# Gates written in place and staged ahead of the residual steps; in the scan, the last states' carry folded in by ScalarE and one product divided by columns

## The chip, the cores and the metric

The kernel runs on one core of a Trainium2 chip. The time is device microseconds (us) of one execution; lower is better. The core's engines are TensorE (PE, with its weight loads as PEld), VectorE (DVE), ScalarE (ACT) and GpSimd (POOL), each with its own queue of instructions in a fixed order, and SyncE (SP), which issues most DMAs. Engines meet only at semaphores.

## The reference

An input x of 2 x 128 x 64 x 64 goes through four layers; the change touches layer 1's end, layer 2 and layer 3.

```python
# layer 1, its end
d = (out - out.mean((2, 3))) ** 2
out = out * sigmoid(d / (4 * (d.sum((2, 3)) / n + 1e-4)) + 0.5) + x      # the gate
# layer 2
for _ in range(3):
    t = relu(conv3x3(x, w1) + b1)
    x = x + (conv3x3(t, w2) + b2) / 3
x = relu(x)
# layer 3: four directions over the pixels (rows, columns, each forward and backward)
dt = softplus(...); dA = exp(dt * A)           # 256 channels x 16 states x 4096 steps
dBu = dt * B * u
h[t] = dA[t] * h[t-1] + dBu[t]                 # the scan
y = sum over states of h * C, + u * D, * silu(z), @ W_out
out = x + fuse(y of the four directions)
```

## The kernel before, in words

**The gate, layer 1 to 2.** `gate` (L918) makes one part of an image: a DMA brings the part of x (`xr`) from `g.xs`, ScalarE does Square (L923) and Sigmoid (L924) into `e`, VectorE multiplies by the fused image (L925), and VectorE (image 0) or GpSimd (image 1) adds x and writes the sum by columns of four into `first` (L926), which lies in the memory of `v[1][b]`. `gated(b, k)` (L1030) calls it for part k of image b (17, 16, 16 and 15 rows), and then `differences` (GpSimd, L1009 and L1010) and `combine` (VectorE, ten operations, L1019 to L1028), which make six transformed inputs `v[0][b]` from the four columns. All four parts of image 0 come first, then `settle(0)` (ScalarE copies `first` to `image`, L1044), `quad_weights` (ten VectorE operations on the second weights) and the residual steps.

**The residual steps, layer 2.** `block(step, j, b, k)` (L1046) is one half image of one convolution: 36 matmuls into six of eight PSUM banks, L1052; then two ScalarE copies, ten VectorE operations (L1060 to L1072), a relu, and the `combine` of the block that went before it (`due`). Step 0, convolution 0 has four such blocks; the gates of image 1 stand behind the blocks of image 0, two parts behind each.

**The scan, layer 3.** 64 blocks (2 images, 4 directions, 8 pieces of 512 steps; called i) each have 8 groups k = (hf, ng): a half of the channels and four of the sixteen states. A group holds four units q, each 128 x 512. In the order of a group: `db_dve` (L1413) and `db_pool` (L1422) make `db` = B times dt*u, VectorE `ND[hf][ng]` of the four units, from PSUM, and GpSimd the rest; `expo` (L1430) is ScalarE's exp into `da`, one of three PSUM banks, two units ahead of the scan (`AHEAD`); `scan` (L1439) is VectorE's scan in place on `db`, whose initial value is the column `hl` that the same group left in the block before, or 0.0 in the first block of a direction; `keep` (L1444, ScalarE) saves the last column to `hl`; `cmul` (L1449, GpSimd) multiplies by C; `sums` (L1457, TensorE) adds up the states. Between groups ScalarE has the work of the next block: two table loads and two silus at the end of slot 7 (L1300, L1301) and of slot 4 (L1313, L1314), two copies at the end of slot 0 (L1325, L1327), softplus at the end of slots 1 and 2. A group's place in its block, 0 to 7, is its slot. All of this is in an order written out by hand (`manual_schedule`).

Of the kernel before, what the change touches and what calls it, by code (L numbers as in the profile page):

```python
# [20 lines left out]
P = 128  # L21
# [925 lines left out]
def layer2(g, I):  # L947
# [14 lines left out]
    with ExitStack() as ctx:  # L962
# [8 lines left out]

        mid = [a.tile([P, 4, RP, NS], F32, name=f"mid{i}") for i in range(2)]

        raw = mid[1].rearrange("p c r i -> p (c r i)")[:, : 9 * P]
        nc.sync.dma_start(raw, I["w2T"].rearrange("p t o -> p (t o)"))
        u2 = a.tile([P, 3, NX, P], F32, name="u2")
        weights = (g.u1, u2)
# [32 lines left out]
            nc.gpsimd.tensor_sub(t[1], d[5], d[3])  # L1010
            return t

        def combine(dst, at, src, r0, n, t):
# [5 lines left out]
            stt(o[2], d[2], -4.0, d[4], ALU.mult, ALU.add)  # L1019
            stt(h, d[1], -4.0, d[3], ALU.mult, ALU.add)  # L1020
            nc.vector.tensor_add(o[1], o[2], h)  # L1021
            nc.vector.tensor_sub(o[2], o[2], h)
            nc.vector.tensor_sub(d42, d[4], d[2])
# [6 lines left out]
        def gated(b, k):  # L1030

            r0, r1 = (0, 17, 33, 49, 64)[k : k + 2]
            n = r1 - r0
            dst = first[b][:, :, r0:r1, 0:NQ]
            if g.gates:
                t = wk.tile([P, 2, 17 * HW], F32, name="gt")
                gate(g, b, r0, n, t[:, 0, : n * HW], t[:, 1, : n * HW], dst, by_column, nc.gpsimd if b else nc.vector)
            else:
                nc.vector.tensor_copy(dst, interior(g, b, r0, n).rearrange("p r (i c) -> p c r i", c=4))
            places = [v[0][b][:, x, 1 + r0 : 1 + r1, :] for x in (0, 5)]  # L1040
            combine(v[0][b], r0, first[b], r0, n, differences(first[b], r0, n, places))

        def settle(b):
            nc.scalar.copy(image[b], first[b])  # L1044

        def block(step, j, b, k):  # L1046
            m = {}
            for x in (1, 2, 3, 4, 0, 5):
                m[x] = ps.tile([P, BLK], F32, name="m")
                for dy in range(3):  # L1050
                    r0 = k * RP + dy
                    nc.tensor.matmul(  # L1052
                        m[x], weights[j][:, dy, x, :], v[j][b][:, x, r0 : r0 + RP, :].rearrange("p r i -> p (r i)"),
                        start=(dy == 0), stop=(dy == 2),
                    )
            s, p = (wk.tile([P, BLK], F32, name=f"m{i}", bufs=2) for i in range(2))
# [12 lines left out]
            stt(d, q, 8.0, d, ALU.mult, ALU.add)  # L1069
            nc.vector.tensor_add(s, s, p)  # L1070
            nc.vector.tensor_add(y[0], rows_of(s), rows_of(m[0]))
            nc.vector.tensor_add(y[3], rows_of(d), rows_of(m[5]))  # L1072
            xv = image[b][:, :, k * RP : (k + 1) * RP, 0:NQ]
            if j == 0:
                nc.scalar.activation(inner(t), inner(t), AF.Relu)
                where = (v[1][b], k * RP, t, 0, RP)
            elif step < 2:
                nc.vector.tensor_add(xv, xv, inner(t))
                where = (v[0][b], k * RP, image[b], k * RP, RP)
            else:  # L1080
# [5 lines left out]
                where = None  # L1086

            if due:
# [6 lines left out]
        with tc.manual_schedule():  # L1095
            for b in range(NB):
                nc.gpsimd.memset(first[b][:, :, :, NQ:], 0.0)
                for e in (0, HP - 1):
                    nc.gpsimd.memset(v[0][b][:, :, e, :], 0.0)
            nc.gpsimd.memset(mid[0][:, :, :, NQ:], 0.0)  # L1100
            for k in range(4):
                gated(0, k)
            settle(0)
            quad_weights(g, u2, raw.rearrange("p (y x o) -> p y x o", y=3, x=3), 1.0 / 3.0)
            nc.gpsimd.memset(mid[1][:, :, :, NQ:], 0.0)
            for step in range(3):
                for j in range(2):
                    for b in range(NB):
                        if step == 0 and j == 0:
                            for e in (0, HP - 1):  # L1110
                                nc.gpsimd.memset(v[1][b][:, :, e, :], 0.0)
                        for k in range(NK):
                            block(step, j, b, k)
                            if step == j == b == 0:
                                gated(1, 2 * k)
                                gated(1, 2 * k + 1)
                        if step == j == b == 0:
                            settle(1)


def layer3(g, I, out):
# [5 lines left out]
    nc, tc = g.nc, g.tc  # L1127
    NJ = 4

    ND = ((4, 0, 1, 4), (4, 4, 0, 4))  # L1130
    NNG = N_STATE // NJ
    HB = 1
    HC = 3
    with ExitStack() as ctx:
# [259 lines left out]

        def copies(i, x, ng):

            if x == "b" and ND[0][ng] == ND[1][ng] == 4:
# [11 lines left out]
        def db_dve(k):  # L1409
            i, hf, ng = groups[k]  # L1410
            n = ND[hf][ng]
            if n:
                nc.vector.tensor_tensor(  # L1413
                    db_tile(k)[:, :n, :], G[k].pop("pb").unsqueeze(1).to_broadcast([P, n, BLK]),
                    S[i]["d4", hf][:, 1, :n, :], ALU.mult,
                )

        def db_pool(k):
            i, hf, ng = groups[k]
            n = ND[hf][ng]  # L1420
            if n < 4:
                nc.gpsimd.tensor_tensor(  # L1422
                    db_tile(k)[:, n:, :], S[i]["b", ng].unsqueeze(1).to_broadcast([P, 4 - n, BLK]),
                    S[i]["d4", hf][:, 1, n:, :], ALU.mult,
                )

        def expo(k, q):
            i, hf, ng = groups[k]
            da = psd.tile([P, BLK], F32, name="da")
            nc.scalar.activation(da, S[i]["d4", hf][:, 0, q, :], AF.Exp, scale=am[:, hf, q, ng : ng + 1])  # L1430
            G[k]["da", q] = da

        def scan(k, q):
            i, hf, ng = groups[k]
            d0, d1 = G[k].pop(("da", q)), G[k]["db"][:, q, :]
            if reverse(i):
                d0, d1 = d0[:, ::-1], d1[:, ::-1]
            first = i % NBLK == 0
            nc.vector.tensor_tensor_scan(d1, d0, d1, 0.0 if first else hl[:, hf, ng, q, :], ALU.mult, ALU.add)  # L1439

        def keep(k):
            i, hf, ng = groups[k]
# [124 lines left out]
        with tc.manual_schedule():  # L1567
# [62 lines left out]
            for k in range(len(groups) + 7):  # L1630
# [221 lines left out]
```

## Time and profile before

| what | value |
|---|---|
| median of 3 runs | 5816.95 us (5814.35 to 5819.41) |
| profiled execution, its own time | 5815.21 us |
| its span, mean granted TensorE clock | 5813.4 us, 0.889 |
| busy: PE, DVE, ACT, POOL | 84%, 76%, 66%, 62% of the span |
| layer 2: first VectorE operation on a gate's sum, last matmul's end | 2017.37 us, 2441.92 us |
| layer 3: first scan, last scan's start | 2500.78 us, 5796.04 us |

A duration is that of one instruction. Two instructions that follow each other on an engine can overlap by some 0.08 to 0.1 us, so what an instruction costs its engine is the time from its start to the next one's. "idle before" is time in which the engine waited, with what ended the wait.

### The profile page before, as it was taken

Reading aid. Unit: us, or ns where it says so; the run is one execution under the profiler, and the core shown is the slowest. Engines: PE = TensorE matmul, PEld = TensorE weight load, DVE = VectorE, ACT = ScalarE, POOL = GpSimd, SP = SyncE. Lnnn points to the kernel's source line nnn. Section 1 sums busy time; section 2 is a strip of 40 time slices with the busy share of each in tenths; the row PEclk is TensorE's granted clock in tenths of the full one; section 3 lists DMA queues with packets and bytes.
Section 4 is the critical chain, followed back from the end, with each engine's and each line's share of the span. In section 5 each row is a group of like instructions: output and inputs, shape, how many; then the busy total and the mean of one; then the engine's idle time right before and its main releaser. Section 6 shows DMA issues by size and latency. Waiting matters only on the chain.

```text
span 5813.4 us, 57554 instructions
## 1 busy us (share of the span) xinstructions
PE 4881.1 (84%) x19110; PEld 1732.0 (30%) x19110; DVE 4427.0 (76%) x4138; ACT 3827.3 (66%) x5499; POOL 3620.8 (62%) x1136
## 2 busy tenths in 40 slices
PE   7999999989978779977787777787788877777776
PEld 3333333334434334422222222222222222222221
DVE  5333333356124589779999999999999999999998
ACT  4888888850025521277777777777777777777775
POOL 5111111110010031179999999999999999999998
PEclk8999999999989889988888888888888888888886
DMA  5000001030046300065555555556655555555554
GB/s 157 19 19 19 19 19 33 1 60 1 1 90 121 74 18 0 6 143 128 135 130 131 143 140 129 128 130 148 145 129 136 127 134 143 139 129 135 132 139 102
DMA packets 333105, 541.88 MB, mean 93 GB/s; under 512 B 66384, under 2 KB 121184, under 8 KB 331712
## 3 DMA queue, kind: packets, MB, share of 16 engines
q1 hardware_dynamic: 329664, 534.58, 39.5%
q10 hardware_dynamic: 3136, 3.56, 0.2%
q8 instruction: 151, 2.47, 0.2%
q14 instruction: 154, 1.26, 0.1%
HBM read 448.81 MB, written 89.13 MB: 93 GB/s over the span
## 4 chain that ended last, share of the span: by engine, by line
DVE 50%; PE 37%; issue 4%; POOL 3%; DMA 3%; ACT 2%; SPq 1%; DVEq 0%; POOLq 0%; ACTq 0%
DVE db L1439 35%; DVE db L1413 11%; PE ps L287 11%; PE acc L303 9%; PE m L1052 6%; PE m L566 5%; PE acd L812 2%; DVE gt L1466 1%; PE m L526 1%; POOL db L1449 1%; POOL db L1422 1%; PE pf L775 1%; PE pc L663 1%; DMA c<-bx 1%; SPq L748 1%
## 5 line engine op out<-in xcount | busy, mean ns | idle before, releaser
L1449 POOL TENSOR_TENSOR db<-db,c 128x2048 f32<-128x2048 f32 x512 | 2310.8, 4532 | 36.5 <-ACT hl L1444 33.8
L1439 DVE TENSOR_TENSOR_SCAN db<-da,hl,db 128x512 f32<-128x512 f32 x1792 | 2154.7, 1263 | 40.4 <-ACT da L1430 3.5
L1430 ACT ACTIVATE da<-dd,am 128x512 f32<-128x512 f32 x2048 | 1402.2, 689 | 803.4 <-DVE db L1439 794.1
L293 ACT ACTIVATE e<-ps 128x1024 f16<-128x1024 f32 x1024 | 992.2, 1021 | 134.5 <-PE ps L287 117.2
L1422 POOL TENSOR_TENSOR db<-b,dd 128x2048 f32<-128x2048 f32 (+1 forms) x192 | 799.8, 4166 | 13.3 <-DMA b<-bx 13.3
L1457 PE MATMUL py<-db,fold 128*32 128x512 f32 x4096 | 618.0, 689 | 223.9 <-POOL db L1449 220.9
L1413 DVE TENSOR_TENSOR db<-pbc,dd 128x2048 f32<-128x2048 f32 (+1 forms) x384 | 766.5, 1996 | 32.0 <-DMA dd<-dx 32.0
L314 DVE RECIPROCAL rec<-acc 32x512 f32<-32x512 f32 x64 | 214.9, 3358 | 639.0 <-PE acc L303 612.1
L321 POOL TENSOR_TENSOR parts<-parts 32x512 f32<-32x512 f32 x64 | 80.4, 1257 | 975.1 <-DVE parts L320 975.1
L287 PE MATMUL ps<-q,k 32*128 32x512 f32 x4096 | 656.0, 643 | 3.5 <-DVE flag L250 2.7
L303 PE MATMUL acc<-e,v 128*128 128x512 f16 x2048 | 531.3, 382 | 0.0
L1052 PE MATMUL m<-v,u 128*128 128x512 f32 x864 | 376.1, 598 | 51.7 <-DVE v L1021 51.7
L1360 PE MATMUL pm<-dd,ident 128*128 128x512 f32 x512 | 356.6, 834 | 2.9 <-ACT dd L1353 2.7
L1392 PE MATMUL pbc<-bc,sel 64*128 64x512 f32 x384 | 207.5, 540 | 153.5 <-DVE db L1413 152.9
L1319 PE MATMUL pm<-u,wxp 128*72 128x512 f32 x256 | 189.4, 882 | 155.2 <-ACT u L1300 155.2
L303 PEld LDWEIGHTS <-v 128*128 128x128 bf16 x2048 | 158.5, 97 | 509.6 <-issue 388.3
L287 PEld LDWEIGHTS ps<-q,k 32*128 32x128 f32 x4096 | 229.7, 183 | 227.9 <-issue 146.2
L1439 DVE TENSOR_TENSOR_SCAN db<-da,db 128x512 f32<-128x512 f32 x256 | 292.3, 1202 | 6.2 <-ACT da L1430 1.3
L1457 PEld LDWEIGHTS py<-db,fold 128*32 128x32 f32 x4096 | 90.5, 114 | 607.0 <-POOL db L1449 356.4
L566 PE MATMUL m<-comb,w 64*128 64x512 f32 (+4 forms) x1296 | 269.9, 575 | 0.0
L1295 PE MATMUL pm<-xt,wcs 128*128 128x512 f32 x512 | 235.6, 602 | 24.6 <-ACT xa L1484 15.4
L686 POOL TENSOR_SCALAR yt<-y 32x512 f32<-32x512 f32 x8 | 18.2, 2271 | 381.7 <-DVE y L677 381.4
(318 smaller groups left out, 6031.8 us busy)
## 6 DMA issues: line engine op xcount, KB each, us to landing
dd<-dx SPq DMA_DIRECT2D x1024, 256.0 KB, 6.4
dx<-dd SPq DMA_DIRECT2D x128, 512.0 KB, 5.4
c<-bx SPq DMA_DIRECT2D x1024, 64.0 KB, 2.1
hats<-pos SPq DMA_DIRECT2D x136, 256.0 KB, 9.5
b<-bx SPq DMA_DIRECT2D x512, 64.0 KB, 4.5
q<-qd SPq DMA_DIRECT2D x32, 512.0 KB, 7.4
w<-in_conv0T SPq DMA_DIRECT2D x18, 288.0 KB, 8.6
q<-in_x SPq DMA_DIRECT2D x8, 512.0 KB, 7.2
```

Source lines behind the costliest of these rows:

```text
L287: nc.tensor.matmul(ps[:, i, :], k4[h % 2][rows, kb // 4, :], q4[h % 2][rows, qb * BLK : (qb + 1) * BLK], start=True, stop=True,)
L293: nc.scalar.activation(e[:, :n, :], ps[:, :n, :], AF.Exp)
L303: nc.tensor.matmul(acc, v3[b][:, kb, h, :], e[:, i, :], start=(kb == 0), stop=(kb == NS - 1))
L566: yield lambda q=q, dy=dy, src=src, i0=i0, i1=i1: nc.tensor.matmul(m[:, i0 * NF : i1 * NF], w[half, dy, q, x, :], src, start=(dy == KC and ...
L1052: nc.tensor.matmul(m[x], weights[j][:, dy, x, :], v[j][b][:, x, r0 : r0 + RP, :].rearrange("p r i -> p (r i)"), start=(dy == 0), stop=(dy ...
L1360: nc.tensor.matmul(ps, g.ident, S[i]["dd", hf][:, x, :], start=(x == 0), stop=(x == 1))
L1413: nc.vector.tensor_tensor(db_tile(k)[:, :n, :], G[k].pop("pb").unsqueeze(1).to_broadcast([P, n, BLK]), S[i]["d4", hf][:, 1, :n, :], ALU.mult,)
L1422: nc.gpsimd.tensor_tensor(db_tile(k)[:, n:, :], S[i]["b", ng].unsqueeze(1).to_broadcast([P, 4 - n, BLK]), S[i]["d4", hf][:, 1, n:, :], ALU ...
L1430: nc.scalar.activation(da, S[i]["d4", hf][:, 0, q, :], AF.Exp, scale=am[:, hf, q, ng : ng + 1])
L1439: nc.vector.tensor_tensor_scan(d1, d0, d1, 0.0 if first else hl[:, hf, ng, q, :], ALU.mult, ALU.add)
L1449: nc.gpsimd.tensor_mul(v, v, S[i]["c", ng].unsqueeze(1).to_broadcast([P, 4, BLK]))
L1457: nc.tensor.matmul(S[i]["y", hf][32 * q : 32 * q + 32, :], fold, G[k]["db"][:, q, :], start=False, stop=(ng == NNG - 1),)
```

## The change

**Layer 1 to 2.** `gate`'s steps become `gate_weight` (the DMA into `gt`; Square and Sigmoid, which now read the image by columns of four and write straight into `first`), `gate_product` (VectorE, in place), `gate_sum` (adds x from `gt`; VectorE for part 0 of image 0, GpSimd for all others), `gate_differences` and `gate_combine`. `combine` takes a `between`: a product of a later part, put behind its fourth operation. `block` is divided into `products` (matmuls), `outputs` and `later` (the `combine` that is due). The order of the first four blocks and the eight parts is written out; `quad_weights` comes behind the third block's outputs. The second weights are loaded into the upper end of `v[1][1]` in place of `mid[1]`. `gate` itself is left for a case that doesn't occur here.

**Layer 3.** For the units q = 2 and 3 of every group, and for all four of the groups whose `db` GpSimd makes alone, except in a direction's first block, ScalarE adds `da[first] * hl` to the first column of `db` right behind `expo`, and the scan starts from 0.0. These are 20 of a block's 32 units, 56 blocks: 1120. `ND` counts columns instead of units: in group (0, 2) VectorE makes columns 0 to 175 of all four units in place of one whole unit. `keep(k - 1)` moves ahead of `expo(k, 2)`.

```diff
-        raw = mid[1].rearrange("p c r i -> p (c r i)")[:, : 9 * P]
+        raw = v[1][1].rearrange("p x r i -> p (x r i)")[:, 4 * HW * NS : 4 * HW * NS + 9 * P]
...
+        at = (0, 17, 33, 49, 64)
+        gt = wk.tile([P, 2, 17 * HW], F32, name="gt")
+        def gate_weight(b, k):
+            r0, n, dst, fu = part(b, k)
+            nc.sync.dma_start(gt[:, k % 2, : n * HW], g.xs[b][:, r0 * HW : (r0 + n) * HW])
+            nc.scalar.activation(dst, fu, AF.Square, bias=g.stat[:, b, 0:1])
+            nc.scalar.activation(dst, dst, AF.Sigmoid, bias=g.half, scale=g.stat[:, b, 1:2])
...
+        def gate_product(b, k):
+            _, _, dst, fu = part(b, k)
+            if g.gates:
+                nc.vector.tensor_mul(dst, dst, fu)
...
+        def gate_sum(b, k, eng):
+            _, n, dst, _ = part(b, k)
+            if g.gates:
+                eng.tensor_add(dst, dst, by_column(gt[:, k % 2, : n * HW]))
...
+            for k in range(2):
+                gate_weight(0, k)
+            gate_product(0, 0)
+            gate_sum(0, 0, nc.vector)
+            gate_product(0, 1)
+            t0 = gate_differences(0, 0)
+            gate_sum(0, 1, nc.gpsimd)
+            t1 = gate_differences(0, 1)
+            gate_weight(0, 2)
+            gate_weight(0, 3)
+            gate_combine(0, 0, t0)
+            gate_combine(0, 1, t1, (0, 2))
+            m00 = products(0, 0, 0)
+            gate_sum(0, 2, nc.gpsimd)
+            t2 = gate_differences(0, 2)
+            gate_weight(1, 0)
+            gate_combine(0, 2, t2, (0, 3))
...
+            w00 = outputs(0, 0, 0, 0, m00)
+            m01 = products(0, 0, 1)
...
+            gate_combine(1, 0, t0, (1, 2))
+            gate_combine(1, 1, t1, (1, 3))
...
+            w01 = outputs(0, 0, 0, 1, m01)
+            m10 = products(0, 1, 0)
+            gate_combine(1, 2, t2)
+            gate_combine(1, 3, t3)
+            settle(1)
+            later(w00)
+            later(w01)
+            w10 = outputs(0, 0, 1, 0, m10)
+            m11 = products(0, 1, 1)
             quad_weights(g, u2, raw.rearrange("p (y x o) -> p y x o", y=3, x=3), 1.0 / 3.0)
...
+            later(w10)
+            later(outputs(0, 0, 1, 1, m11))
...
-    ND = ((4, 0, 1, 4), (4, 4, 0, 4))
+    ND = ((BLK, 0, 176, BLK), (BLK, BLK, 0, BLK))
...
-                    db_tile(k)[:, n:, :], S[i]["b", ng].unsqueeze(1).to_broadcast([P, 4 - n, BLK]),
-                    S[i]["d4", hf][:, 1, n:, :], ALU.mult,
+                    db_tile(k)[:, :, n:], S[i]["b", ng][:, n:].unsqueeze(1).to_broadcast([P, 4, BLK - n]),
+                    S[i]["d4", hf][:, 1, :, n:], ALU.mult,
...
+        def carried(k, q):
+            i, hf, ng = groups[k]
+            return i % NBLK > 0 and (q >= 2 or ND[hf][ng] == 0)
         def expo(k, q):
...
+            if carried(k, q):
+                first = BLK - 1 if reverse(i) else 0
+                b0 = G[k]["db"][:, q, first : first + 1]
+                nc.scalar.activation(b0, da[:, first : first + 1], AF.Identity, bias=b0, scale=hl[:, hf, ng, q, :])
...
-            nc.vector.tensor_tensor_scan(d1, d0, d1, 0.0 if first else hl[:, hf, ng, q, :], ALU.mult, ALU.add)
+            zero = i % NBLK == 0 or carried(k, q)
+            nc.vector.tensor_tensor_scan(d1, d0, d1, 0.0 if zero else hl[:, hf, ng, q, :], ALU.mult, ALU.add)
...
+                    if q == 0 and ended:
+                        keep(k - 1)
                     if 4 * k + q + AHEAD < len(units):
                         expo(*units[4 * k + q + AHEAD])
...
-                    if q == 0 and ended:
-                        keep(k - 1)
```

More of the change, by code (lines that the diff above doesn't have):

```diff
@@ L1011, in differences, with combine @@
             return t
-        def combine(dst, at, src, r0, n, t):
+        def combine(dst, at, src, r0, n, t, between=None):
             d = columns_of(src, r0, n)
@@ L1022, in combine @@
             nc.vector.tensor_sub(o[2], o[2], h)
+            if between:
+                gate_product(*between)
             nc.vector.tensor_sub(d42, d[4], d[2])
@@ L1028, in combine, with part, gate_differences, gate_combine @@
             stt(o[5], d31, -4.0, t[1], ALU.mult, ALU.add)
[L1030 to L1034, printed above, removed]
-            if g.gates:
-                t = wk.tile([P, 2, 17 * HW], F32, name="gt")
-                gate(g, b, r0, n, t[:, 0, : n * HW], t[:, 1, : n * HW], dst, by_column, nc.gpsimd if b else nc.vector)
-            else:
-                nc.vector.tensor_copy(dst, interior(g, b, r0, n).rearrange("p r (i c) -> p c r i", c=4))
-            places = [v[0][b][:, x, 1 + r0 : 1 + r1, :] for x in (0, 5)]
-            combine(v[0][b], r0, first[b], r0, n, differences(first[b], r0, n, places))
+        at = (0, 17, 33, 49, 64)
+        gt = wk.tile([P, 2, 17 * HW], F32, name="gt")
+        def part(b, k):
+            r0, r1 = at[k : k + 2]
+            return r0, r1 - r0, first[b][:, :, r0:r1, 0:NQ], interior(g, b, r0, r1 - r0).rearrange("p r (i c) -> p c r i", c=4)
+        def gate_weight(b, k):
+            r0, n, dst, fu = part(b, k)
+            if g.gates:
+                nc.sync.dma_start(gt[:, k % 2, : n * HW], g.xs[b][:, r0 * HW : (r0 + n) * HW])
[5 more added lines that the diff above has]
+                nc.vector.tensor_mul(dst, dst, fu)
+            else:
+                nc.vector.tensor_copy(dst, fu)
+        def gate_sum(b, k, eng):
+            _, n, dst, _ = part(b, k)
+            if g.gates:
+                eng.tensor_add(dst, dst, by_column(gt[:, k % 2, : n * HW]))
+        def gate_differences(b, k):
+            r0, n, _, _ = part(b, k)
+            return differences(first[b], r0, n, [v[0][b][:, x, 1 + r0 : 1 + r0 + n, :] for x in (0, 5)])
+        def gate_combine(b, k, t, between=None):
+            r0, n, _, _ = part(b, k)
+            combine(v[0][b], r0, first[b], r0, n, t, between)
         def settle(b):
             nc.scalar.copy(image[b], first[b])
-        def block(step, j, b, k):
+        def products(j, b, k):
             m = {}
@@ L1055, in block, with outputs @@
                     )
+            return m
+        def outputs(step, j, b, k, m):
             s, p = (wk.tile([P, BLK], F32, name=f"m{i}", bufs=2) for i in range(2))
@@ L1086, in block, with later @@
                 where = None
+            return where
+        def later(where):
             if due:
@@ L1099, in layer2 @@
                     nc.gpsimd.memset(v[0][b][:, :, e, :], 0.0)
-            nc.gpsimd.memset(mid[0][:, :, :, NQ:], 0.0)
-            for k in range(4):
-                gated(0, k)
-            settle(0)
+            for t in mid:
+                nc.gpsimd.memset(t[:, :, :, NQ:], 0.0)
+            for k in range(2):
[5 more added lines that the diff above has]
+            gate_sum(0, 1, nc.gpsimd)
@@ new lines, in layer2 @@
+            t1 = gate_differences(0, 1)
[8 more added lines that the diff above has]
+            gate_combine(0, 2, t2, (0, 3))
+            gate_sum(0, 3, nc.gpsimd)
+            t3 = gate_differences(0, 3)
+            gate_weight(1, 1)
+            gate_combine(0, 3, t3, (1, 0))
@@ new lines, in layer2 @@
+            settle(0)
+            gate_sum(1, 0, nc.gpsimd)
+            t0 = gate_differences(1, 0)
+            gate_weight(1, 2)
+            gate_product(1, 1)
+            w00 = outputs(0, 0, 0, 0, m00)
+            m01 = products(0, 0, 1)
+            gate_sum(1, 1, nc.gpsimd)
+            t1 = gate_differences(1, 1)
+            gate_weight(1, 3)
+            for e in (0, HP - 1):
+                nc.gpsimd.memset(v[1][0][:, :, e, :], 0.0)
+            gate_combine(1, 0, t0, (1, 2))
+            gate_combine(1, 1, t1, (1, 3))
@@ L1104, in layer2 @@
+            gate_sum(1, 2, nc.gpsimd)
+            t2 = gate_differences(1, 2)
+            gate_sum(1, 3, nc.gpsimd)
+            t3 = gate_differences(1, 3)
+            w01 = outputs(0, 0, 0, 1, m01)
[7 more added lines that the diff above has]
+            m11 = products(0, 1, 1)
             quad_weights(g, u2, raw.rearrange("p (y x o) -> p y x o", y=3, x=3), 1.0 / 3.0)
-            nc.gpsimd.memset(mid[1][:, :, :, NQ:], 0.0)
+            for e in (0, HP - 1):
+                nc.gpsimd.memset(v[1][1][:, :, e, :], 0.0)
@@ L1108, in layer2 @@
                     for b in range(NB):
-                        if step == 0 and j == 0:
-                            for e in (0, HP - 1):
-                                nc.gpsimd.memset(v[1][b][:, :, e, :], 0.0)
                         for k in range(NK):
[L1113 to L1118, printed above, removed]
+                            if step or j:
+                                later(outputs(step, j, b, k, products(j, b, k)))
 def layer3(g, I, out):
@@ L1395, in copies @@
         def copies(i, x, ng):
-            if x == "b" and ND[0][ng] == ND[1][ng] == 4:
+            if x == "b" and ND[0][ng] == ND[1][ng] == BLK:
                 return
@@ L1413, in db_dve @@
                 nc.vector.tensor_tensor(
-                    db_tile(k)[:, :n, :], G[k].pop("pb").unsqueeze(1).to_broadcast([P, n, BLK]),
-                    S[i]["d4", hf][:, 1, :n, :], ALU.mult,
+                    db_tile(k)[:, :, :n], G[k].pop("pb")[:, :n].unsqueeze(1).to_broadcast([P, 4, n]),
+                    S[i]["d4", hf][:, 1, :, :n], ALU.mult,
                 )
@@ L1420, in db_pool @@
             n = ND[hf][ng]
[L1421 removed]
+            if n < BLK:
                 nc.gpsimd.tensor_tensor(
[L1423 to L1425 removed]
+                    db_tile(k)[:, :, n:], S[i]["b", ng][:, n:].unsqueeze(1).to_broadcast([P, 4, BLK - n]),
+                    S[i]["d4", hf][:, 1, :, n:], ALU.mult,
+                )
+        def carried(k, q):
+            i, hf, ng = groups[k]
+            return i % NBLK > 0 and (q >= 2 or ND[hf][ng] == 0)
         def expo(k, q):
@@ L1437, in scan @@
                 d0, d1 = d0[:, ::-1], d1[:, ::-1]
-            first = i % NBLK == 0
-            nc.vector.tensor_tensor_scan(d1, d0, d1, 0.0 if first else hl[:, hf, ng, q, :], ALU.mult, ALU.add)
+            zero = i % NBLK == 0 or carried(k, q)
+            nc.vector.tensor_tensor_scan(d1, d0, d1, 0.0 if zero else hl[:, hf, ng, q, :], ALU.mult, ALU.add)
         def keep(k):
```

## The prediction

> **What bounds the kernel now.** I read the page first, then busy time by windows, then the timelines of the engines in the two places that the change touches, and the chain of waits between them. In layer 3 VectorE and GpSimd are both near full (a block of a direction's first piece, then a later one; columns: window, length, busy us of PE, PEld, DVE, ACT, POOL, granted clock, DMA):
>
> ```profile
> 4978.70:5028.30 49.60, 39.89 (x121) 12.17 (x121) 49.00 (x40) 37.91 (x63) 48.86 (x14) 0.85 0.59 139
> 5028.30:5079.90 51.60, 41.36 (x122) 12.66 (x121) 50.94 (x41) 37.74 (x63) 51.60 (x14) 0.80 0.58 135
> ```
>
> Which of the two sets the pace is seen in what differs between these blocks. Only the first's scans start from 0.0 and need no `hl` (VectorE's timeline, start, length of all, count):
>
> ```profile
> 4978.72 9.02 DVE L1439 TENSOR_TENSOR_SCAN db<-da,db 128x512 f32<-128x512 f32 x8
> ```
> ```profile
> 5028.34 9.51 DVE L1439 TENSOR_TENSOR_SCAN db<-da,hl,db 128x512 f32<-128x512 f32 x8
> ```
>
> From start to start a scan takes 1.115 us without `hl` and 1.175 with it: 0.060 more. For 32 scans that is 1.92 us, and the blocks' starts are 49.62 and 51.54 apart, 1.92 as well. The period follows VectorE alone. GpSimd's own work in a block, start to start, is ten products at 4.48 us, one at 3.40 (1536 columns) and two at 1.23: 50.7, less than 51.54. ScalarE is busy 38 us of 51.5, but in lumps. The tightest one stands between slots 7 and 0 (ScalarE's timeline):
>
> ```profile
> 4050.59 0.69 ACT L1430 ACTIVATE da<-dd,am 128x512 f32<-128x512 f32 x1 [0.48 <-DVE db L1439]
> 4051.30 1.28 ACT L1300 ACT_TABLE_LOAD   x1
> 4052.59 1.26 ACT L1300 ACTIVATE u<-pm,vecs 128x512 f32<-128x512 f32 x2
> 4053.88 1.28 ACT L1301 ACT_TABLE_LOAD   x1
> 4055.17 0.69 ACT L1430 ACTIVATE da<-dd,am 128x512 f32<-128x512 f32 x1
> 4055.80 0.18 ACT L1444 COPY hl<-db 128x4 f32<-128x4 f32 x1
> 4055.89 1.31 ACT L1430 ACTIVATE da<-dd,am 128x512 f32<-128x512 f32 x2
> 4057.68 0.69 ACT L1430 ACTIVATE da<-dd,am 128x512 f32<-128x512 f32 x1 [0.48 <-DVE db L1439]
> 4058.31 0.57 ACT L1325 COPY xd<-pm 72x512 f32<-72x512 f32 x1
> 4058.79 0.56 ACT L1327 CAST bc<-pm 32x512 fp32r<-32x512 f32 x1
> 4059.26 0.68 ACT L1430 ACTIVATE da<-dd,am 128x512 f32<-128x512 f32 x1
> ```
>
> The exp of 4055.17 is unit 2 of slot 0 and ends at 4055.86; its scan, third in a row that starts at 4054.02, begins at 4056.37: 0.51 us to spare. The exp of 4059.26 is unit 2 of slot 1, needed at 4061.07.
>
> In layer 2 TensorE runs without a gap from 2115.78 to 2441.92, 21 half images at 15.53 us; before that, from 2017, it waits for VectorE (the longest three waits of its matmuls are 51.7 us on L1021). There VectorE and GpSimd hinder each other (timeline of all engines, GpSimd's L1009 and L1010 beside VectorE's `combine`):
>
> ```profile
> 2104.04 0.42 DVE L1019 SCALAR_TENSOR_TENSOR v<-v 128x256 f32<-128x256 f32 x1 [5.15 <-POOL v L926]
> 2104.09 0.87 POOL L1009 TENSOR_TENSOR v<-v 128x256 f32<-128x256 f32 x1
> 2104.39 0.86 DVE L1020 SCALAR_TENSOR_TENSOR t<-v 128x256 f32<-128x256 f32 x1
> ...
> 2106.49 0.42 DVE L1023 TENSOR_TENSOR t<-v 128x256 f32<-128x256 f32 x1
> ```
>
> An operation of 0.42 us takes 0.86 beside GpSimd.
>
> **The scan, step by step.** (1) 1120 scans lose 0.060 us each on VectorE, the engine that sets the pace: -67.2. The instruction lists show 672 scans with `hl` left, so the change does what it says. (2) In group (0, 2) VectorE makes 4 x 176 = 704 columns instead of 512. Its rows for 2048 and 512 (2.366 and 0.767 start to start) give 1.04 ns a column: 0.20 us x 64 = +12.8. GpSimd has 1344 columns instead of 1536, 0.41 less: 50.3 a block, below what VectorE needs below, so nothing is gained or lost there. Every scan of this group now needs GpSimd's share, where unit 0 was VectorE's alone; at the median that scan began 0.03 us before GpSimd's end, and with 0.41 less it is covered; if GpSimd lags, it waits.
>
> (3) ScalarE gets 1120 operations of 128x1 with two pointer operands and a wait on its own exp. No row shows one. Nearest are `keep` (128x4, no pointer, 0.18) and L835 (128x2 from PSUM, one pointer, 0.26). A second pointer costs 0.09 (L924 with two 1.24, L923 with one 1.15, 1024 columns). I take 0.35, between 0.18 and an outer 0.55. The wait on the exp is 0.03 (from L1354's end to L1355's start). A carried unit thus takes 0.69 + 0.03 + 0.35 - 0.09 of overlap = 0.98 us, still below a scan's 1.115, and on average ScalarE has room: 38 + 20 x 0.36 = 45 of 51. But behind the lump at 4051.30 five carried units come in a row (slot 0 units 2 and 3, slot 1 units 0 to 2), with the two copies (0.95) before the last. `keep` first, 0.09: unit 2 of slot 0 is ready at 4055.17 + 0.09 + 0.69 + 0.03 + 0.35 + 0.04 for the semaphore = 4056.37, needed at 4056.31 (one scan before it is shorter). Three more at 0.98, copies 0.95, `keep` 0.09, the last 0.98: 4061.33, needed at 4061.07 - 5 x 0.06 = 4060.77. VectorE waits 0.56 us in each of 56 blocks: +31.4. Where these operations wait for `db` (they stand behind `db_dve` in 307 cases and GpSimd's product in 140), the next exp in ScalarE's queue waits for a later scan anyway. The other lumps leave more: slot 4's had 0.71 us before, and after it nothing but units.
>
> The Trainium skill (ScalarE: Activation LUTs, section What ACT_TABLE_LOAD costs) gives an activation 186 ns plus 0.833 per column, and some 93 more for each pointer operand. By it the new operation takes 0.373, the wait grows by 5 x 0.023 to 0.68, and the scan's gain shrinks by 6.4 us; `da`'s row of 0.69 with one pointer agrees with it (0.71).
>
> (4) `keep` ahead of `expo` lets GpSimd's product start up to 0.6 earlier; GpSimd waits for it only 31.9 us in all and is not the bound: 0. Sum of layer 3: -67.2 + 12.8 + 31.4 = -23.0.
>
> **The gates.** (5) The first gate's Square and Sigmoid no longer stand between layer 1's last silus: the chain of waits shows there 1.09 us at 1999.56 and 3.90 from 2003.49 to 2007.39, with two table loads. Layer 1 ends 5.0 earlier, at 2012.3. Then they stand at the front: Square now reads by fours; L1259, which reads with a stride, takes 1.10 against 0.57, so 2.3 for 1.19; table 1.28, Sigmoid 1.29: first product at 2017.2, as late as the first sum before (2017.37).
>
> (6) From there VectorE and GpSimd share what follows, since both read two inputs from SBUF. Per part: product, one input by fours, between 1.22 (L925) and 2.0 (L926 on VectorE, both by fours); I take 2.0, as L855 pays 1.10 for 0.69 with one strided. Sum on GpSimd between 2.2 (half of L1449) and 4.02 (L926); I take 3.1, one of two inputs by fours. `combine` 3.7 and differences 1.2 without hindrance. Part (0, 0) 9.0 with its sum on VectorE, seven parts 10.0, two outputs 12.1, less 2.5 where a sum lies under operations that read PSUM: `combine` (1, 3) ends at 2105.8. Then the due `combine` 6.1, the third outputs 6.1, `quad_weights` 5.2, differences beside them 1.8, three operations of the next `combine` 2.0: the fifth half image starts at 2127.0, against 2115.78 + 15.53 = 2131.3. TensorE has no gap from there: -4.3. With 4.02 for the sums it is +2, with 1.22 and 2.2 it is -17.
>
> The Trainium skill (SBUF — State Buffer, section Who interferes with whom) says that a VectorE operation with two SBUF inputs and a GpSimd one that reads SBUF exclude each other for a whole instruction. It speaks against moving sums to GpSimd to run beside `combine`. The 0.86 above agrees; were the seven sums hidden, the gates would give 22 us more.
>
> **Sum.** -23.0 - 4.3 = -27.3 from the profiled 5815.2: 5787.9. The median of the runs lies 1.7 above the profiled time: 5789.6, and I say 5790.
>
> **Rivals.** *ScalarE keeps up.* If the new operation costs 0.24 or less, its row then nearer L835, the wait of 0.56 is gone (5 x 0.11): 5817 - 54.4 - 4.3 = 5758, and 5745 with cheap gates. For it: ScalarE's average load. *No change to be measured.* At 0.43 the wait is 0.96, 53.8 a run, and dear gates give back 2: 5818. *Slower: ScalarE becomes the bound.* Every 0.01 us beyond 0.35 costs 5 x 0.01 x 56 = 2.8 us. It decides from 0.45; at 0.55 VectorE waits 1.56 a block, 87.4 us, and the time is 5817 - 54.4 + 87.4 - 4.3 = 5846. For it: the operation waits for the exp just issued, and 447 of them for a second semaphore. Against: the 0.03 of L1354 to L1355, and L835.
>
> **Chances.** Forecast 0.46 (5772 to 5804), ScalarE keeps up 0.27, no change 0.17, slower 0.10. The range 5752 to 5818 leaves out the slower case and the far end of the fast one. A measurement tells about 0.2% (11.6 us) from no change: faster 0.46 + 0.27 + 0.04 of the third case, same 0.13, slower 0.10.
>
> **What would show it.** The scan's two rows: 672 at 1.26 and 1376 at 1.20 us. A row of 1120 at 128x1: 0.35 means the forecast, 0.26 the fast rival, 0.45 the slow one. VectorE's idle time ahead of slot 1's third scan, ended by that row, about 31 us in all. GpSimd's 4x336 product at 3.0. The last matmul of layer 2 at about 2437.6. I am wrong if later blocks' starts are not about 51.1 apart, or if VectorE waits for GpSimd instead.

## The result, and the profile after

The changed kernel takes 5788.69 us, median of 5 runs (5785.89 to 5790.97), against 5816.95 (5 runs, 5811.51 to 5819.41): ratio 0.9953, 95% interval 0.9942 to 0.9964. Predicted were 5790, between 5752 and 5818. Its profiled span is 5785.8 us against 5813.4, at a granted clock of 0.890 against 0.889.

The new rows on the page of the changed kernel (columns: line, engine, operation, out<-in, count, busy us and mean ns of one, idle us before it and what ended most of that). L1516 is the carry, L1524 the scan, L1488 `db_dve`:

```profile
L1524 DVE TENSOR_TENSOR_SCAN db<-da,db 128x512 f32<-128x512 f32 x1376 | 1585.0, 1203 | 34.6 <-ACT db L1516 26.6
L1524 DVE TENSOR_TENSOR_SCAN db<-da,hl,db 128x512 f32<-128x512 f32 x672 | 825.9, 1271 | 40.3 <-POOL db L1497 3.0
L1488 DVE TENSOR_TENSOR db<-pbc,dd 128x2048 f32<-128x2048 f32 (+1 forms) x384 | 781.0, 2034 | 31.7 <-DMA dd<-dx 31.7
L1516 ACT ACTIVATE db<-da,db,hl 128x1 f32<-128x1 f32 x1120 | 393.7, 352 | 147.3 <-DVE db L1488 103.8
```

The carry costs 0.352, where 0.35 was taken. The estimate of 0.373 from the Trainium skill's figures (ScalarE: Activation LUTs, section What ACT_TABLE_LOAD costs) is 0.02 too high for this shape; the row decides. The scans without `hl` lose 26.6 us to it; of those with `hl` the largest single releaser is GpSimd's product with 3.0.

The same two blocks as before, a direction's first and a later one (busy time by windows; window, length, PE, PEld, DVE, ACT, POOL, granted clock, DMA):

```profile
4956.75:5006.61 49.86, 39.76 (x122) 12.52 (x121) 49.21 (x40) 37.97 (x63) 49.82 (x14) 0.85 0.59 139
5006.61:5057.78 51.17, 42.33 (x122) 13.35 (x121) 50.11 (x40) 43.45 (x83) 50.98 (x14) 0.80 0.57 136
```

A later block, where the carry is at work, takes 51.17 instead of 51.55. A direction's first block, which carries nothing, takes 49.86 instead of 49.62: the product by columns alone. VectorE is now busy only 50.11 of 51.17, and its timeline says where the rest is:

```profile
5006.61 2.46 DVE L1524 TENSOR_TENSOR_SCAN db<-da,hl,db 128x512 f32<-128x512 f32 x2
5009.03 4.57 DVE L1524 TENSOR_TENSOR_SCAN db<-da,db 128x512 f32<-128x512 f32 x4
5013.99 2.34 DVE L1524 TENSOR_TENSOR_SCAN db<-da,db 128x512 f32<-128x512 f32 x2 [0.40 <-ACT db L1516]
```

The wait stands ahead of the seventh scan, slot 1's unit 2. From start to start this scan's predecessor takes 1.595 instead of 1.115: 0.48 lost (the view counts 0.40, as it starts at the end of the scan before). ScalarE's timeline of the same stretch, with five carried units and the two copies (not all lines are shown):

```profile
5006.53 1.28 ACT L1376 ACT_TABLE_LOAD   x1
5007.82 0.20 ACT L1529 COPY hl<-db 128x4 f32<-128x4 f32 x1
5007.92 0.69 ACT L1510 ACTIVATE da<-dd,am 128x512 f32<-128x512 f32 x1
5008.64 0.35 ACT L1516 ACTIVATE db<-da,db,hl 128x1 f32<-128x1 f32 x1
5008.90 0.68 ACT L1510 ACTIVATE da<-dd,am 128x512 f32<-128x512 f32 x1
...
5011.85 0.57 ACT L1400 COPY xd<-pm 72x512 f32<-72x512 f32 x1
5012.32 0.57 ACT L1402 CAST bc<-pm 32x512 fp32r<-32x512 f32 x1
5012.80 0.19 ACT L1529 COPY hl<-db 128x4 f32<-128x4 f32 x1
5012.89 0.68 ACT L1510 ACTIVATE da<-dd,am 128x512 f32<-128x512 f32 x1
5013.61 0.35 ACT L1516 ACTIVATE db<-da,db,hl 128x1 f32<-128x1 f32 x1
```

ScalarE has no idle time here: exp to exp is 0.98 (5007.92 to 5008.90), and the last carry ends at 5013.96, 0.03 before the scan that needs it.

In the gates, VectorE and GpSimd in the stretch where one of the moved sums runs (timeline of all engines, TensorE's rows left out):

```profile
2032.78 0.42 DVE L1025 TENSOR_TENSOR t<-v 128x256 f32<-128x256 f32 x1
2032.94 2.94 POOL L1059 TENSOR_TENSOR v<-v,gt 128x1024 f32<-128x1024 f32 x1 [4.95 <-DVE v L1052]
2033.11 3.05 DVE L1026 TENSOR_TENSOR t<-v 128x256 f32<-128x256 f32 x1
```

Two instructions of the same shape, one behind the other: 0.42, and 3.05 beside GpSimd's sum. Six of the seven sums on GpSimd hold a VectorE operation up like this (to 2.90 to 3.14); the seventh lies mostly beside operations that read PSUM, which take 0.68 to 0.69 as without it. It fits what the Trainium skill states (SBUF — State Buffer, section Who interferes with whom), that a VectorE operation with two SBUF inputs contends with a GpSimd one that reads SBUF, for ports that one of them holds alone: the VectorE operation ends 0.28 behind the GpSimd one. Even so layer 2 is done earlier: its last matmul ends at 2429.4 (2441.9 before), and the first scan starts at 2488.1 (2500.8).

### The profile page after: what moved, and what is told of

The parts are those of the page before. It is cut to its first block, busy times and chain, and to the rows that moved or that the text cites. A ratio compares the mean times of both kernels' runs of the same rounds, so it can differ in the third digit from the quotient of the medians.

```text
span 5785.8 us, 58630 instructions
## 1 busy us (share of the span) xinstructions
PE 4889.5 (85%) x19110; PEld 1740.4 (30%) x19110; DVE 4400.7 (76%) x4135; ACT 4153.4 (72%) x6617; POOL 3602.9 (62%) x1139
## 4 chain that ended last, share of the span: by engine, by line
DVE 42%; PE 38%; ACT 10%; issue 5%; DMA 2%; POOL 2%; SPq 1%; DVEq 0%; POOLq 0%; ACTq 0%
DVE db L1524 28%; PE ps L287 11%; DVE db L1488 10%; PE acc L303 9%; PE m L1078 5%; PE m L566 5%; ACT da L1510 3%; PE acd L812 2%; ACT db L1516 1%; DVE gt L1551 1%; PE m L526 1%; ACT L1375 1%; ACT u L1375 1%; PE pf L775 1%; POOL db L1534 1%
## 5 line engine op out<-in xcount | busy, mean ns | idle before, releaser
L1534 POOL TENSOR_TENSOR db<-db,c 128x2048 f32<-128x2048 f32 x512 | 2313.2, 4533 | 45.4 <-ACT hl L1529 31.4
L1524 DVE TENSOR_TENSOR_SCAN db<-da,db 128x512 f32<-128x512 f32 x1376 | 1585.0, 1203 | 34.6 <-ACT db L1516 26.6
L1524 DVE TENSOR_TENSOR_SCAN db<-da,hl,db 128x512 f32<-128x512 f32 x672 | 825.9, 1271 | 40.3 <-POOL db L1497 3.0
L1488 DVE TENSOR_TENSOR db<-pbc,dd 128x2048 f32<-128x2048 f32 (+1 forms) x384 | 781.0, 2034 | 31.7 <-DMA dd<-dx 31.7
L1497 POOL TENSOR_TENSOR db<-b,dd 128x2048 f32<-128x2048 f32 (+1 forms) x192 | 773.2, 4027 | 13.0 <-DMA b<-bx 13.0
L1542 PE MATMUL py<-db,fold 128*32 128x512 f32 x4096 | 600.7, 672 | 151.8 <-POOL db L1534 151.8
L1516 ACT ACTIVATE db<-da,db,hl 128x1 f32<-128x1 f32 x1120 | 393.7, 352 | 147.3 <-DVE db L1488 103.8
L1394 PE MATMUL pm<-u,wxp 128*72 128x512 f32 x256 | 182.7, 855 | 141.4 <-ACT u L1375 141.4
```

Source lines behind the costliest of these rows:

```text
L1488: nc.vector.tensor_tensor(db_tile(k)[:, :, :n], G[k].pop("pb")[:, :n].unsqueeze(1).to_broadcast([P, 4, n]), S[i]["d4", hf][:, 1, :, :n], A ...
L1497: nc.gpsimd.tensor_tensor(db_tile(k)[:, :, n:], S[i]["b", ng][:, n:].unsqueeze(1).to_broadcast([P, 4, BLK - n]), S[i]["d4", hf][:, 1, :, n ...
L1516: nc.scalar.activation(b0, da[:, first : first + 1], AF.Identity, bias=b0, scale=hl[:, hf, ng, q, :])
L1524: nc.vector.tensor_tensor_scan(d1, d0, d1, 0.0 if zero else hl[:, hf, ng, q, :], ALU.mult, ALU.add)
L1534: nc.gpsimd.tensor_mul(v, v, S[i]["c", ng].unsqueeze(1).to_broadcast([P, 4, BLK]))
L1542: nc.tensor.matmul(S[i]["y", hf][32 * q : 32 * q + 32, :], fold, G[k]["db"][:, q, :], start=False, stop=(ng == NNG - 1),)
```

## The experiments

Each of the twelve kernels was timed in several rounds beside the kernel before on the same chip, whose medians were 5815 to 5818 there. Line numbers are those of the changed kernel, unless said; in E7 they are one or two higher. Code and rows are excerpts.

Two kinds of block are kept apart below. In or just before blocks 1 to 5 and 22 to 30 the layer norm of pixels still to come is worked on too; these are called the 14 blocks with a layer norm (13 carried ones, and block 24, a direction's first; block 0 is left out). The other carried blocks, without the last one of all, are the 42 plain blocks. A block's time is that from its first scan's start to the next block's. The sum of the 14 differs by up to 1.7 us between traces of the same layer 3 (733.6, 734.7 and 735.3 in the changed kernel, E2 and E8).

**One part at a time.** E1 has the gates of layers 1 and 2 alone, E2 layer 3's change alone.

> The kernel before with the change of layer 1 and 2 alone. Theory read from the changed kernel's trace: the gates bring nearly half of the gain, since its first scan starts 12.7 us earlier; 12.7 less than before, 5804. The prediction's own sum: 4.3 less, 5813. Rival (the gates bring nothing, all comes from the scans): 5817, first scan at 2500.8.

Measured: 5804.33, ratio 0.9980 (0.9971 to 0.9989), 10.9 less.

> The kernel before with the change of layer 3 alone. Theory: VectorE sets the pace, saves 20 x 0.056 us in a carried block and loses 0.48 there to ScalarE's row of carried units and 0.23 to the wider product; the stretch of the scans is 14.5 shorter, 5802. The prediction's own sum: 23.0 less, 5794. Rival (the gates gave the whole gain): 5817.

Measured: 5800.41, ratio 0.9972 (0.9960 to 0.9983), 14.8 less; from the first scan to the last one 3280.2 us against 3295.3. So both halves bring something, and the gates more than twice what the prediction gave them, the scans two thirds.

**Within the scan.** E3 and E4 take the parts of E2 apart, both with the saved columns' copy in its old place.

```diff
 # E3: columns, no carry
...
-    ND = ((4, 0, 1, 4), (4, 4, 0, 4))
+    ND = ((BLK, 0, 176, BLK), (BLK, BLK, 0, BLK))
...
 # E4: carry, units
+            if carried(k, q):
...
+                nc.scalar.activation(b0, da[:, first : first + 1], AF.Identity, bias=b0, scale=hl[:, hf, ng, q, :])
```

> The kernel before with the product of group (0, 2) divided by columns, and nothing else: no carry, the old place of the saved columns. Theory (VectorE sets the pace): slower by 64 x 0.20 to 0.23, so 12.8 to 15 us, 5830 to 5832; GpSimd has 0.41 less to do in a block and that is worth nothing. Rival (GpSimd sets the pace): faster by 64 x 0.41 = 26, 5791. Third case: the scan of unit 0, which was VectorE's alone, waits for GpSimd's share, and it is slower by more than 15.

Measured: 5834.61, ratio 1.0034 (1.0021 to 1.0046), 19.4 slower. A plain block takes 51.78 instead of 51.55 and has no new wait: 0.23 for 192 columns more. GpSimd's shorter product is worth nothing here. In the blocks with a layer norm it costs more than the 0.23 (740.8 us for 14 blocks, 734.3 before): there VectorE's scans wait 5.1 us for GpSimd's `db` at slot 2's first unit, and before 1.5 at its second. That is the third case, in these blocks alone.

> The kernel before with the carry on ScalarE alone: units divided as before, the old place of the saved columns. Theory: 56 x (20 x 0.056 = 1.12 saved, some 0.4 to 0.5 waited at slot 1's unit 2) = 35 to 40 less, 8 less where a layer norm hides it: 28 to 36 less, 5781 to 5789, and so faster than the changed kernel's layer 3 part by the wider product. Rival (without the shorter product GpSimd becomes late now that scans are shorter: 50.7 us of its own work in a block, against VectorE's 51.0): VectorE waits for GpSimd, the gain is under 25 and idle time ended by GpSimd's product grows by over 10 us.

Measured: 5792.99, ratio 0.9959 (0.9945 to 0.9972), 22.2 less, by less than expected. A plain block takes 50.84, 0.71 less, nearly as the theory has it (1.12 saved, 0.45 waited). But a direction's second block takes 0.3 to 0.5 more, the wait standing at slot 2's unit 1, which needs GpSimd's share, and the 14 blocks with a layer norm gain nothing (735.6). Of the rival's two signs the first holds, a gain under 25, and the second fails: VectorE's scans wait 4.8 us for GpSimd's `db`, 1.4 before, and not 10 more. E3 and E4 together make 2.8 less, E2 has 14.8. By the stretch from the first scan to the last in the traces it is 6.2 for 15.1. The medians' intervals (7 to 8 us to each side for each of the three) are too wide to tell how much is missing; it was looked for in E6.

**The row at slot 1.** E5 is the changed kernel with three carried units in ScalarE's row instead of five.

```diff
-            return i % NBLK > 0 and (q >= 2 or ND[hf][ng] == 0)
+            return i % NBLK > 0 and (q >= 2 or (hf, ng) == (1, 2))
```

> The changed kernel, but the first two units of group (0, 1), which stands at slot 1, read hl in the scan again, so ScalarE's row behind the lump has three carried units instead of five. Theory (VectorE waits 0.48 us there because the row is late by what these operations cost): the wait at slot 1's unit 2 is gone, two scans cost 0.06 more each, 0.36 less in each of the 42 plain carried blocks and something in the 14 with a layer norm: 15 to 26 us less, 5763 to 5774. Rival (the wait comes from something else, such as the two copies or VectorE's own product): the wait stays, and it is 56 x 0.12 = 7 slower, 5796.

Measured: 5775.44, ratio 0.9930 (0.9917 to 0.9944): 13 below the changed kernel, 1.4 above the range expected. VectorE's timeline in the same block as above:

```profile
4994.34 2.46 DVE L1524 TENSOR_TENSOR_SCAN db<-da,hl,db 128x512 f32<-128x512 f32 x2
4996.76 2.34 DVE L1524 TENSOR_TENSOR_SCAN db<-da,db 128x512 f32<-128x512 f32 x2
4999.01 2.43 DVE L1524 TENSOR_TENSOR_SCAN db<-da,hl,db 128x512 f32<-128x512 f32 x2
5001.36 2.31 DVE L1524 TENSOR_TENSOR_SCAN db<-da,db 128x512 f32<-128x512 f32 x2
```

Two more scans read `hl` again, and no idle time stands ahead of the seventh. The 42 plain blocks together take 15.5 us less, 0.37 each. So the wait was the row's length. The 14 blocks with a layer norm gain nothing (734.7): there something else is late.

**The copy's place.** E6 puts `keep` behind `expo` again in the changed kernel.

> The changed kernel with the saved columns' copy in its old place, behind the exp and the carry. The prediction's step (4): no difference, but unit 2 of slot 1 is ready 0.09 earlier, 0.39 waited instead of 0.48: 5 us less at most, 5784 to 5789. Rival (the copy's place is what lets the divided product and the carry go together, since both alone gave 3 less and together 15 less): about 9 to 12 us slower, 5798 to 5800, lost in the blocks with a layer norm.

Measured: 5794.05, ratio 0.9963 (0.9950 to 0.9977): some 5 slower than the changed kernel, between the two expectations (3.3 by the traces, from the first scan to the last). The plain blocks are 0.09 faster, which is the copy's own time in ScalarE's row; the 14 with a layer norm are 6.3 us slower together, most of it at slot 2's first unit: VectorE's scans wait 13.1 us for GpSimd's `db`, and 3.4 in the changed kernel. A direction's first blocks are slower too, by 0.2 each. So the copy's new place is worth 3 to 5 us, through GpSimd, and explains less than half of what E3 and E4 left open; the rest stays open.

**A dearer carry.** E7 adds to the changed kernel a second operation of the same shape behind each carry, written to a column that nobody reads.

```diff
...
+                nc.scalar.activation(spare, da[:, first : first + 1], AF.Identity, bias=vec(g, "ln_b"), scale=hl[:, hf, ng, q, :])
```

> The changed kernel with a second operation of 128x1 with two pointers behind each carried exp, written to a column that nobody reads: the price of a carried unit is higher by its start-to-start time of 0.26 to 0.35 us. The slower rival of the prediction (each 0.01 us costs 2.8 us because ScalarE's row of five sets the pace): 73 to 98 us slower, 5862 to 5887, with VectorE's wait at slot 1's unit 2 at 1.8 to 2.2 us. Against it (ScalarE has slack elsewhere and VectorE's wait does not grow with the price): under 30 slower.

Measured: 5886.11, ratio 1.0122 (1.0107 to 1.0138): 97 above the changed kernel. VectorE's timeline in the block of the windows above:

```profile
5079.72 2.46 DVE L1526 TENSOR_TENSOR_SCAN db<-da,hl,db 128x512 f32<-128x512 f32 x2
5082.38 4.91 DVE L1526 TENSOR_TENSOR_SCAN db<-da,db 128x512 f32<-128x512 f32 x4 [0.20 <-ACT spare L1518]
5088.30 2.43 DVE L1526 TENSOR_TENSOR_SCAN db<-da,db 128x512 f32<-128x512 f32 x2 [1.01 <-ACT spare L1518]
```

The operation costs ScalarE 0.24 from start to start, and the plain block is 1.79 longer. Five of them give 1.2; the rest is new waits, at slot 0's unit 2 and in the carried groups of slots 5 and 6. The expected wait of 1.8 to 2.2 in one place was wrong: it is shared among several. The slower rival was real, and its price of 2.8 us for each 0.01 was too low, since it counts the row of five alone (24 x 2.8 = 67, and 97 measured): the operation's own 0.35 kept it away.

**The sums' engine.** E8 is the changed kernel with all eight gate sums on VectorE.

```diff
-            gate_sum(0, 1, nc.gpsimd)
+            gate_sum(0, 1, nc.vector)
...
```

> The changed kernel with all eight gate sums on VectorE instead of one. Theory (a sum on GpSimd blocks VectorE for its whole 2.9 us, so that seven cost VectorE some 18 to 20; on VectorE they cost 2.15 each, 15): the last matmul of layer 2 is 2 to 5 us earlier, 5783 to 5787. Rival (the sums on GpSimd lie hidden beside operations that read PSUM or wait): seven times 2.15 are added to VectorE's chain, 10 to 15 us slower, 5799 to 5804.

Measured: 5784.63, ratio 0.9946 (0.9932 to 0.9960), 4 below the changed kernel. From layer 1's end to layer 2's last matmul its trace has 414.4 us, and six traces with the sums on GpSimd 417.7 to 419.3. VectorE's timeline, as above in the gates:

```profile
2032.83 0.42 DVE L1026 TENSOR_TENSOR t<-v 128x256 f32<-128x256 f32 x1
...
2034.63 2.03 DVE L1059 TENSOR_TENSOR v<-v,gt 128x1024 f32<-128x1024 f32 x1
```

The operation of 3.05 is back at 0.42, and the sum costs VectorE 2.03. So moving these sums to GpSimd saved VectorE nothing: for six of the seven it paid 2.5 to 2.7 in waiting for about 2.0 of work.

**The blocks with a layer norm.** In these 14 blocks the change gained next to nothing (734.3 before, 733.6 after), where 13 plain ones gain 4.9. TensorE's timelines of the changed kernel tell part of the reason, in such a block (first scan at 3827.02) and in a plain one (first scan at 5006.61):

```profile
3828.36 2.08 PE L1292 MATMUL da<-xa,onesm 128*128 128x512 f32 x2 [4.68 <-DVE db L1524]
3830.22 2.54 PE L1394 MATMUL pm<-u,wxp 128*72 128x512 f32 x4
```
```profile
5005.98 3.49 PE L1394 MATMUL pm<-u,wxp 128*72 128x512 f32 x4 [2.68 <-ACT u L1375]
```

The norm's mean (L1292) waits for a `da` buffer, that is for VectorE's first scan, and stands ahead of the projection (L1394) in TensorE's queue. ScalarE's two copies wait for the projection, which starts 3.2 us after the first scan instead of 0.6 ahead of it. E10 puts the projection first, on E5:

```diff
+                if norm and slot == 0:
+                    front_pe(i + 1, slot)
                 for q in range(4):
...
-                front_pe(i + 1, slot)
+                if not (norm and slot == 0):
+                    front_pe(i + 1, slot)
```

> The kernel with the shorter row, and in the blocks with a layer norm the projection's matmuls (L1394 there) stand ahead of the mean's matmul (L1292) in TensorE's queue. Theory: in these 14 blocks the mean waits for VectorE's first scan to free a buffer of da, the projection behind it comes 3.8 us later than in a plain block, ScalarE's two copies come 1.9 us later, and VectorE waits up to 1.4 us at slot 1's unit 2 whatever the scans cost; so these blocks gained nothing from the carry. With the projection first the 14 blocks take 8 to 14 us less (720 to 727 instead of 734.7), the time is 5762 to 5768. Rival (these blocks are held by the layer norm's own work on ScalarE or VectorE, such as the wait of the subtraction for the mean): under 4 us, 5772 to 5776.

Measured: 5767.61, ratio 0.9911 (0.9896 to 0.9926), 8 below E5. The 14 blocks take 728.7, 6.0 less: between theory and rival, though the time lies in the theory's range. Of VectorE's waits in E5, the 8.5 us for the carry are gone, and those for GpSimd's `db` have grown from 5.2 to 7.8. TensorE's timeline there:

```profile
3821.58 3.69 PE L1394 MATMUL pm<-u,wxp 128*72 128x512 f32 x4 [3.12 <-ACT u L1375]
3825.06 1.92 PE L1292 MATMUL da<-xa,onesm 128*128 128x512 f32 x2
```

E12 does the same to the kernel before.

> The kernel before with the projection ahead of the mean in the layer norm blocks and nothing else. Theory: before the change these blocks already lost 6.9 us to waits, so at most 7 less, 5809 to 5815, against 8 to 14 where scans are shorter: the loss grew as the carry took work from VectorE. Rival: as much as with the shorter row or nothing.

Measured: 5812.03, ratio 0.9991 (0.9982 to 1.0000), 5 less, at the edge of what can be told; by the trace the 14 blocks take 2.5 less. So this loss seems to have been there before, but smaller: a faster VectorE made it larger. The order is only part of the matter. With the projection first in both, E5's row gains 3.9 in the 13 carried blocks with a layer norm (681.4 in E12, 677.5 in E10), where 13 plain ones gain 9.9 (51.55 to 50.79). Without that order it gained nothing. Some of what is left is VectorE's longer wait for GpSimd's `db` (7.8 in E10, 3.9 in E12); the rest was not taken apart.

**All together.** E11 has E5's row, E10's order and E8's sums; E13 is E11 with group (0, 2) divided by units again.

> The changed kernel with the shorter row, the projection first and all gate sums on VectorE. If the three are independent: 5788.7 - 13.3 - 4 and the 0 to 14 of the projection: 5757 to 5771. If one of them lives of another's wait: about as fast as the best of them.

Measured: 5764.33, ratio 0.9908 (0.9892 to 0.9923): below both kernels, 24 below the changed one. Of the 25 that the three gave singly nearly all is there.

> The kernel with the shorter row, the projection first and all gate sums on VectorE (5764.3), but the product of group (0, 2) divided by units again, so VectorE makes 512 columns and GpSimd 1536. If VectorE still set the pace, a plain block would take 50.79 - 0.23 = 50.56 and the time would be about 15 less, 5750. If GpSimd sets it, whose own work is then 50.7 a block, a plain block takes 50.66 to 50.75, VectorE's scans wait for GpSimd's products, and the time is 5756 to 5762. If the division by columns brings something else in the blocks with a layer norm (alone with the carry it seemed to), it is no faster than 5764.

Measured: 5765.44, ratio 0.9912 (0.9895 to 0.9928), as fast as E11. GpSimd's product with C and the scans with `hl` on E11's page, then on E13's:

```profile
L1534 POOL TENSOR_TENSOR db<-db,c 128x2048 f32<-128x2048 f32 x512 | 2312.7, 4533 | 23.5 <-ACT hl L1529 16.4
L1524 DVE TENSOR_TENSOR_SCAN db<-da,hl,db 128x512 f32<-128x512 f32 x784 | 962.3, 1269 | 44.3 <-POOL db L1497 7.6
```
```profile
L1534 POOL TENSOR_TENSOR db<-db,c 128x2048 f32<-128x2048 f32 x512 | 2308.9, 4527 | 3.9 <-ACT hl L1529 3.9
L1524 DVE TENSOR_TENSOR_SCAN db<-da,hl,db 128x512 f32<-128x512 f32 x784 | 967.9, 1270 | 51.3 <-POOL db L1497 10.1
```

GpSimd's product had 23.5 us of idle time before it in E11 (45.4 in the changed kernel) and has 3.9 here, and scans wait longer for GpSimd, now in plain and first blocks too. A plain block takes 50.79 in both, once because VectorE has no gap, once because GpSimd has next to none. The time is that of the third case, but not for its reason: the 14 blocks with a layer norm take 727.3, and 727.8 in E11. The division by columns thus moves work from a full engine to another that is as full.

## Why the prediction was right, step by step

The total is 1.3 us off, but two errors cancel in it: layer 3 gained less than the sum said, the gates more.

*Step (1), the scans.* A plain block's 32 scans took 37.78 us, and take 14.29 with `hl` and 22.37 without (the wait taken out): 1.12 less, where 20 x 0.060 = 1.20 was said. In 56 blocks it is 62.7 for 67.2. The difference of the two forms holds nearly; as medians of single scans 1.175 and 1.115 left out those behind a product or a group's end.

*Step (2), the columns.* VectorE's products take 0.27 more in a carried block and 0.24 in a first one, 17.0 for 12.8. E3 shows 0.23 in a plain block: 192 columns at 1.2 ns, not 1.04. GpSimd's 1344 columns take 3.03, and VectorE waits for GpSimd's `db` 3.4 us in all (1.4 before), next to nothing, as said.

*Step (3), the carry on ScalarE.* This was the critical one, and it held: 0.352 for 0.35, a wait of 0.48 for 0.56, in the place named, in every plain block. E5 took the wait away, E7 made it larger. By the traces VectorE's waits in layer 3, counted from start to start, grow from 7.8 to 38.2, by 30.4; 31.4 was said. But this agreement is partly luck: 20.5 are the waits predicted, in the 42 plain blocks, and 9.4 lie in the 14 with a layer norm, of which the prediction said nothing. It costed each of the 56 blocks as a plain one. In those 14 TensorE's queue, and ScalarE's copies behind it, end last (E10), and then GpSimd for some of the time; what is saved on the scans there mostly lengthens a wait.

*Step (4), the copy.* It was costed at 0; E6 shows a gain of 3 to 5, most of it in just those blocks, where VectorE's scans wait for GpSimd.

Together: -62.7 + 17.0 + 30.4 = -15.3 where -23.0 was said; the trace has 14.5 less from the first to the last scan, and E2 14.8.

*Step (5), layer 1's tail.* From the start of layer 1's last L812 matmul to the end of its last VectorE operation (L967), five traces with the old gates have 43.9 us on average (43.1 to 44.9) and nine with the new ones 38.9 (38.3 to 40.0): 4.9 less, 5.0 said. The first product runs 4.8 after layer 1's end, 4.9 said.

*Step (6), the parts.* From there to layer 2's last matmul, 425.3 on average in those five (424.4 to 426.1) became 418.2 in the six with the change's own sums (417.7 to 419.3): 7.1 less, where the sum said 0.7 more. This is the step that was mis-sized. The terms were near (product 1.9 to 2.2 for 2.0, sum 2.8 to 3.05 for 3.1, and 3.5 for the one of 17 rows), but the prediction laid them end to end, and in the trace parts of a `combine` run beside GpSimd: the products of parts (0, 2), (0, 3) and (1, 0) start 9.1 and 8.8 apart, where 10.0 was said for a part. The first product to the end of `combine` (1, 3) took 85.2 and not 88.6, and the fifth half image, which would start at 2127.0, started in two pieces:

```profile
2115.41 1.95 PE L1078 MATMUL m<-v,u 128*128 128x512 f32 x4 [0.32 <-DVE u L938]
2120.14 80.07 PE L1078 MATMUL m<-v,u 128*128 128x512 f32 x182 [2.77 <-DVE v L1021]
```

(TensorE's timeline of the changed kernel; the second row is cut by the window's end.) It is the second row's start, 110.0 after layer 1's end, where the sum has 114.7; four of its matmuls ran ahead.

Of the rivals, *ScalarE keeps up* failed on the row's price, *no change* on that and on the gates; *slower* is what E7 built.

## What to carry to other kernels

An engine's average room says little for work that is added in front of a consumer: count the longest row of instructions behind the last lump and compare its pace with the consumer's, here 0.98 against 1.115 with a start that was already late. Cost a saving per kind of block, since in those where another engine ends last it becomes a longer wait. And a sum moved to a second engine saves nothing where it holds the first one up for its whole length, as six of seven did here; only moving it back showed it, since the kernel was faster all the same.

## What the runs showed of the hardware

The start of layer 1's last L812 matmul lies between 1970.2 and 1979.0 us in the fourteen traces, though nothing ahead of it differs. A difference of two single traces read at absolute times thus holds up to 9 us that the edit did not make: of the 12.7 by which the changed kernel's first scan is earlier, 2.2 were there at that matmul already. Stretches counted from such a common instruction repeat within some 2 us here. Why the earlier layers vary so was not looked for.

A VectorE operation of 0.42 us can take 3.05 beside one GpSimd sum of 2.94, although the two touch different parts of an image; in the gates of the profile before, the longest such delay was a product of 1.22 that took 2.10, beside a GpSimd operation of 1.40.
